# A four-layer graph network on one core: the last layer with narrow tiles in three bfloat16 parts and six blocks from streamed rows

## The chip, the core and the metric

The kernel runs on one core of a Trainium2 chip. Its engines work side by side, each through its own list of instructions in order: TensorE (PE, with its weight loads shown apart as PEld), VectorE (DVE), ScalarE (ACT), GpSimd (POOL) and SyncE (SP), which only issues transfers. The metric is device time of one execution in microseconds (us), as the median of several runs.

## What is computed

Four layers work on the same 2708 x 2708 adjacency matrix (sparse, densest in the first rows and columns, the diagonal always set) and on 2708 x 512 features. Each adds its result to its input and normalizes every row. The change lies in the last one:

```
bw = sign(weight)                     # 512 x 512
ba = maximum(sign(x), 0)              # 2708 x 512
xw = ba @ bw.T                        # small whole numbers
out = relu(adj @ xw)
x = layernorm(x + out)
```

`xw` holds whole numbers up to 512, which float16 holds exactly. `adj` is float32; the product `adj @ xw` is to keep its precision.

## The kernel before

The rows of the output are cut into 22 blocks of 128 (block 21 has 20). A block's columns of the transposed adjacency matrix are the stationary operands of its matmuls (128 source nodes x 128 output rows), the 512 features the moving ones. Since the matrix is sparse, layer 0 lists for every block, while it reads the matrix, which nodes have an edge to it. The listed rows are packed, 128 to a tile, and kept in SBUF for all layers (`packed[b]`, `tiles(b)` of them), together with index lists (`index[b]`). In each layer POOL then gathers the 128 feature rows of each packed tile from DRAM by an indirect transfer (`gathered`, L611). `ROOM[b]` is the number of gathered tiles of a block, 98 over blocks 1 to 21; `DIRECT[b]` names the blocks of nodes (0 and 1) that a block takes whole, without a list. Block 0 takes all nodes.

Some packed tiles are narrow. `SPLIT[b]` says how: in a block of kind "QQ" the first four gathered tiles hold only edges to one quarter of the block's rows each (32 rows), in "HH" the first two to one half each (64), "QH" and "HQ" have two quarters and one half. `span(b, i)` (L1326) gives the rows of tile i, `narrow_views` (L1343) the packed columns that matter, `whole_runs` (L1331) the runs of neighbouring tiles of full width, `in_turns` (L1360) the order "full width first, narrow last", and `last_of` (L1373) whether a matmul is the last one to its rows. Layers 0 to 2 use these: a narrow tile's matmul writes only the partitions `ps[r0:r1]`. The last layer before the change uses none of them and multiplies every tile at full width.

The last layer (from L1987) has two kinds of blocks. Blocks 0 to `WHOLE3` - 1 = 4 are summed over all 22 tiles of nodes: `whole_tile(j)` (L2060) loads 128 rows of `xw` and the first `W3` = 640 columns of the same rows of the transposed matrix (`aw`, four buffers), and adds to five PSUM banks (`whole`). The other blocks, in the order `order3` = 21, 5, 6, ... 20, are gathered: their tiles of `xw` come by `gather3(b)` (L2048) as float16 rows in DRAM that the transfer widens to float32r, into 11 buffers.

PE multiplies in float32r[...]. So a matrix tile is split by `halves_of` (L1994) into a high part (a cast on ACT, L1998) and the remainder (a subtraction on DVE, L1999), up to 512 columns at a time, `W3` for a streamed tile, in four buffers `parts`; every tile takes two matmuls (L2075 streamed, L2114 packed). The diagonal of a gathered block is added by two more (L2103), with a scaled identity matrix split in the same way (L2095, L2098) and the block's own rows (`xo`, L2087). `widened` (L2004) turns float16 rows into float32r, on ACT two times of three, else on DVE.

`finish3` (L2016) takes a block's sum: relu and addition of the input (L2022, which frees the PSUM bank), moments (L2024, L2026), and for two blocks at a time the inverse root and the scaling (L642 to L662, L2033 to L2043), and the store on SP.

The program text sets the order: five streamed tiles first (`AHEAD3`), then block by block; a counter `due` grows by `ROOM[b]`, and for each three gathered tiles (`FETCHES3`) one streamed tile follows the block. With the values before, the last of the 22 streamed tiles follows block 15. From then on each gathered block is finished together with a streamed one; what is left of these is finished after block 20. A scheduler may move an instruction ahead of others on its engine when the text's order is built, and then the order is fixed.

In layer 2, `gathered_2` (L1784) also uses memory that is no longer needed as places for gathered rows, one after another: two in `packed[0]`, and as many as fit in `early`, the tile that holds `packed[1]` to `packed[WHOLE3 - 1]`, once those blocks are done.

Of the kernel before, what the change touches and what calls it, by code (L numbers as in the profile page):

```python
# [8 lines left out]
F32 = mybir.dt.float32  # L9
# [10 lines left out]
P = 128  # L20
# [36 lines left out]
)  # L57


WHOLE3 = 5  # L60
AHEAD3 = 5
FETCHES3 = 3

# [444 lines left out]
def sparse_layers(ctx, tc, x, adj, adj_t, w0_t, b0, w_sa, a_sa, w_gcnb, b_gcnb, wa, ba, wb, bb, w3_t,  # L508
# [19 lines left out]
    def rows(b: int) -> int:  # L528
        return min(P, N - b * P)

    def direct(b: int):

        return tuple(range(NB)) if b == 0 else DIRECT.get(b, ())

    def tiles(b: int) -> int:
        return len(direct(b)) + ROOM[b]
# [71 lines left out]
    def own_by_itself(b: int) -> bool:  # L608
        return b not in direct(b)

    def gathered(pool, dst_w: int, src, b: int, i: int, dtype=F32):  # L611
        t = pool.tile([P, dst_w], dtype, tag="xg", name=f"xg{b}_{i}")
        nc.gpsimd.indirect_dma_start(  # L613
            out=t, out_offset=None, in_=src[:, :],
            in_offset=bass.IndirectOffsetOnAxis(ap=index[b][:, i : i + 1], axis=0),
        )
        return t
# [708 lines left out]
    def span(b: int, i: int):  # L1326

        t, spans = i - len(direct(b)), SPANS[SPLIT[b]]
        return spans[t][1:] if 0 <= t < len(spans) else (0, rows(b))
# [30 lines left out]
    def in_turns(b: int):  # L1360

        nd, n = len(direct(b)), narrow(b)
        mine = list(range(nd, nd + n))
        return [i for i in range(tiles(b)) if i not in mine] + mine
# [8 lines left out]
    def last_of(b: int, i: int, order):  # L1373

        r0, r1 = span(b, i)
        return all(
            span(b, j)[1] <= r0 or span(b, j)[0] >= r1 for j in order[order.index(i) + 1 :]
        )
# [607 lines left out]

    with tc.tile_pool(name="s_l3", bufs=11, reuse_waits="tile") as lp, \  # L1987
            tc.tile_pool(name="s_ps_w", bufs=1, reuse_waits="tile", space=PSUM) as ps_w, \
            tc.tile_pool(name="s_ps_3", bufs=3, reuse_waits="tile", space=PSUM) as ps_3:
        W3 = WHOLE3 * P  # L1990
        CH3 = 4
        PW = max(CH3 * P, W3)

        def halves_of(a, r: int, w: int, name: str):  # L1994

            p = lp.tile([P, 2, PW], F32R, tag="parts", name=f"p{name}", bufs=4)
            low, high = p[:r, 0, :w], p[:r, 1, :w]
            nc.scalar.copy(high, a)  # L1998
            nc.vector.tensor_tensor(low, a, high.bitcast(F32), op=ALU.subtract)  # L1999
            return p  # L2000

        turn = [0]

        def widened(t, r: int, name: str, tag: str = "wide", bufs: int = 4):  # L2004

            g = lp.tile([P, D], F32R, tag=tag, name=f"w{name}", bufs=bufs)
            turn[0] += 1
            if turn[0] % 3 == 0:
                nc.vector.tensor_copy(g[:r], t[:r])
            else:  # L2010
                nc.scalar.copy(g[:r], t[:r])
            return g

        moments = []

        def finish3(b: int, ps, more: bool):  # L2016

            m = rows(b)
            old = place_of_x(b)
            k = len(moments)  # L2020
            t = old[:, :D]
            nc.vector.scalar_tensor_tensor(t[:m], ps[:m], 0.0, t[:m], op0=ALU.max, op1=ALU.add)  # L2022
            st = small.tile([P, 6], F32, tag="st", name=f"st_3_{b}")
            nc.vector.bn_stats(st[:m], t[:m])  # L2024
            mv = moments[0][2] if k else lp.tile([P, 2, 2], F32, tag="mv3", name=f"mv_3_{b}", bufs=3)
            nc.vector.bn_aggr(mv[:m, k, :], st[:m])  # L2026
            moments.append((b, t, mv))
            if more:
                return
            n = len(moments)  # L2030
            rs = lp.tile([P, 2, 2], F32, tag="rs3", name=f"rs_3_{b}", bufs=2)
            mean, v = mv[:m, :n, 0], mv[:m, :n, 1]
            nc.vector.tensor_scalar(v, v, LN_EPS, None, op0=ALU.add)  # L2033
            rsqrt_of(rs[:m, 0, :n], v, m, n, f"3_{b}")
            nc.vector.scalar_tensor_tensor(
                rs[:m, 1, :n], mean, -1.0, rs[:m, 0, :n], op0=ALU.mult, op1=ALU.mult
            )
            for k, (b, t, _) in enumerate(moments):
                nc.scalar.activation(
                    t[:m], t[:m], AF.Identity, bias=rs[:m, 1, k : k + 1],  # L2040
                    scale=rs[:m, 0, k : k + 1],
                )
                nc.sync.dma_start(out[b * P : b * P + m, :], t[:m])  # L2043
            moments.clear()

        sources3 = {}

        def gather3(b: int):  # L2048
            sources3[b] = [gathered(lp, D, xw_rows, b, t, F32R) for t in range(ROOM[b])]

        order3 = [NB - 1, *range(WHOLE3, NB - 1)]
        gather3(order3[0])
        gather3(order3[1])


        whole = [ps_w.tile([P, D], F32, tag=f"w{b}", name=f"l3_{b}") for b in range(WHOLE3)]

        xw_direct = {0: xw0}

        def whole_tile(j: int):  # L2060
            r = rows(j)
            if j:
                g = lp.tile([P, D], F16, tag="xs", name=f"xs{j}", bufs=4)
                nc.sync.dma_start(g[:r], xw_rows[j * P : j * P + r, :])
                g = widened(g, r, f"s{j}", "wide" if j > 1 else "wide1", 4 if j > 1 else 1)
                if j == 1:
                    xw_direct[1] = g
            else:
                g = xw0
            a = lp.tile([P, W3], F32, tag="aw", name=f"aw{j}", bufs=4)  # L2070
            nc.sync.dma_start(a[:r], adj_t[j * P : j * P + r, :W3])
            p = halves_of(a[:r], r, W3, f"w{j}")
            for b in range(WHOLE3):
                for h in range(2):
                    nc.tensor.matmul(  # L2075
                        whole[b], p[:r, h, b * P : (b + 1) * P], g[:r, :],
                        start=(j == 0 and h == 0), stop=(j == NB - 1 and h == 1),
                    )
        j = 0
        while j < AHEAD3:  # L2080
            whole_tile(j)
            j += 1
        due = 0
        for at, b in enumerate(order3):
            m = rows(b)
            xo = lp.tile([P, D], F16, tag="xo", name=f"xo{b}", bufs=2)
            nc.sync.dma_start(xo[:m], xw_rows[b * P : b * P + m, :])  # L2087
            xo = widened(xo, m, f"o{b}")
            if at + 1 < len(order3) and at:
                gather3(order3[at + 1])  # L2090
            src = [xw_direct[j] for j in direct(b)] + sources3.pop(b)
            ps = ps_3.tile([P, D], F32, tag="mm", name=f"l3_{b}")

            dp = lp.tile([P, 2, P], F32R, tag="dp", name=f"dp{b}", bufs=2)
            nc.scalar.activation(  # L2095
                dp[:m, 1, :m], ident[:m, :m], AF.Copy, scale=dia_own[:m, b : b + 1]
            )
            nc.vector.scalar_tensor_tensor(  # L2098
                dp[:m, 0, :m], ident[:m, :m], dia_own[:m, b : b + 1],
                dp[:m, 1, :m].bitcast(F32), op0=ALU.mult, op1=ALU.subtract,  # L2100
            )
            for h in range(2):
                nc.tensor.matmul(  # L2103
                    ps[:m], dp[:m, h, :m], xo[:m, :], start=(h == 0), stop=False
                )
            for i0 in range(0, tiles(b), CH3):
                n = min(CH3, tiles(b) - i0)
                p = halves_of(
                    packed[b][:, i0 : i0 + n, :].rearrange("p n i -> p (n i)"), P, n * m,
                    f"{b}_{i0}",  # L2110
                )
                for i in range(n):
                    for h in range(2):
                        nc.tensor.matmul(  # L2114
                            ps[:m], p[:, h, i * m : (i + 1) * m], src[i0 + i],
                            start=False, stop=(i0 + i == len(src) - 1 and h == 1),
                        )
            pending = bool(moments)
            finish3(b, ps, not pending and b not in (order3[0], order3[-1]))
            if j == NB and whole and len(moments) == 1:  # L2120
                finish3(WHOLE3 - len(whole), whole.pop(0), False)
            due += ROOM[b]
            while j < NB and due >= FETCHES3:
                whole_tile(j)
                j += 1
                due -= FETCHES3
        while whole:
            finish3(WHOLE3 - len(whole), whole.pop(0), len(whole) % 2 == 1)
# [77 lines left out]
```

## Time and profile before

| | us |
|---|---|
| median of 3 runs | 1006.92 (1006.87 to 1007.9) |
| profiled execution | 1015.66 |
| its span, first to last instruction | 1013.9 |
| layer 2, 580 to 889 us of the span | 309 |
| last layer, 889 us to the end | 124.9 |
| PE busy over the span | 867.5 |
| DVE | 654.6 |
| ACT | 381.2 |
| POOL | 513.0 |

Durations of single instructions come from the profiled execution, which is 8.7 us longer than the median. "Busy" is the time in which an engine runs an instruction; matmuls overlap in the records, so their cost is read from the distance between starts. The "idle before" of an instruction names what its engine waited for last; "issue" is a wait for nothing that the profile shows, and can be a transfer.

The lines of the page that are the last layer's costliest:

```profile
L2075 PE MATMUL l<-ws,pw 128*128 128x512 f32 (+1 forms) x210 | 52.0, 401 | 3.7 <-DVE pw L1999 3.7
L2075 PEld LDWEIGHTS l<-ws,pw 128*128 128x128 f32 (+1 forms) x210 | 40.4, 194 | 14.0 <-DVE pw L1999 4.6
L613 POOL DMA_INDIRECT xg<-xw_rows,i x70 | 71.4, 1020 | 39.9 <-issue 16.5
```

Columns: line, engine, operation, tile written and tiles read, shapes, count; then busy time and mean ns of one; then the engine's idle time just before them and its main cause.

### The profile page before, as it was taken

Reading aid. Unit: us, or ns where it says so; the run is one execution under the profiler, and the core shown is the slowest. Engines: PE = TensorE matmul, PEld = TensorE weight load, DVE = VectorE, ACT = ScalarE, POOL = GpSimd, SP = SyncE. Lnnn points to the kernel's source line nnn. Section 1 sums busy time; section 2 is a strip of 40 time slices with the busy share of each in tenths; the row PEclk is TensorE's granted clock in tenths of the full one; section 3 lists DMA queues with packets and bytes.
Section 4 is the critical chain, followed back from the end, with each engine's and each line's share of the span. In section 5 each row is a group of like instructions: output and inputs, shape, how many; then the busy total and the mean of one; then the engine's idle time right before and its main releaser. Section 6 shows DMA issues by size and latency. Waiting matters only on the chain.

```text
span 1013.9 us, 12803 instructions
## 1 busy us (share of the span) xinstructions
PE 867.5 (86%) x3659; PEld 458.7 (45%) x3659; DVE 654.6 (65%) x2538; ACT 381.2 (38%) x822; POOL 513.0 (51%) x579
## 2 busy tenths in 40 slices
PE   1888889659587977989999988998999999699983
PEld 0444444212122324455555544453555555378762
DVE  5889797717366863546455436666888777556765
ACT  2665555100000012545445433333444333254654
POOL 2677888567666533646434034453454320066761
PEclk9898889879798988999999998999999999889986
DMA  9999895467676634766645266676786551299985
GB/s 288 332 330 313 293 299 162 142 197 215 189 228 202 199 122 132 216 198 207 199 150 165 80 235 239 225 272 219 261 320 224 176 176 44 82 308 331 310 233 169
DMA packets 93557, 220.06 MB, mean 217 GB/s; under 512 B 13660, under 2 KB 28364, under 8 KB 93476
## 3 DMA queue, kind: packets, MB, share of 16 engines
q0 software_dynamic: 43008, 127.61, 42.1%
q1 hardware_dynamic: 38520, 76.78, 22.3%
q10 hardware_dynamic: 11948, 14.76, 4.4%
q8 instruction: 31, 0.51, 0.2%
q14 instruction: 50, 0.41, 0.1%
HBM read 178.21 MB, written 31.71 MB: 207 GB/s over the span
## 4 chain that ended last, share of the span: by engine, by line
PE 63%; DVE 15%; issue 6%; DMA 6%; another core or an unknown queue 5%; ACT 3%; POOL 1%; ACTq 0%; DVEq 0%; SPq 0%; POOLq 0%
PE l L1369 11%; PE h L1595 7%; PE e L1820 6%; PE a L1820 6%; PE l L2075 4%; PE y L1106 4%; PE pg L1868 4%; PE l L2114 3%; PE pc L1868 3%; DMA xg<-x_rows,i 2%; PE e L1628 2%; PE px L1929 2%; PE a L1629 2%; DVE s_mask L874 1%
## 5 line engine op out<-in xcount | busy, mean ns | idle before, releaser
L613 POOL DMA_INDIRECT xg<-x_rows,i x98 | 94.8, 967 | 113.4 <-PE l L1369 65.7
L1072 POOL DMA_INDIRECT a<-in_adj_t_dram,row_at x98 | 111.0, 1132 | 59.2 <-DVE deg L817 24.0
L613 POOL DMA_INDIRECT xg<-y_rows,i x98 | 97.5, 995 | 50.3 <-issue 21.8
L1106 PE MATMUL y<-s_w,xt 128*128 128x512 f32 (+1 forms) x176 | 96.8, 702 | 0.0
L1369 PE MATMUL l<-xg,a 128*32 128x512 f32 (+3 forms) x196 | 83.2, 657 | 12.1 <-DMA xg<-y_rows,i 11.8
L613 POOL DMA_INDIRECT xg<-xw_rows,i x70 | 71.4, 1020 | 39.9 <-issue 16.5
L1796 POOL DMA_INDIRECT xg<-x_rows,i x60 | 59.9, 999 | 61.8 <-ACT ae L1551 18.0
L1595 PE MATMUL h<-s_wsa,xt 128*128 128x256 f32 (+3 forms) x352 | 83.5, 391 | 5.2 <-ACT xt L1590 5.0
L1796 POOL DMA_INDIRECT a<-x_rows,i x38 | 36.9, 970 | 93.3 <-DVE mask L1554 38.0
L1595 PEld LDWEIGHTS h<-s_wsa,xt 128*128 128x128 f32 (+1 forms) x352 | 65.4, 190 | 30.6 <-ACT xt L1590 14.0
L809 ACT ACTIVATE unused<-arow 128x1408 uint8<-128x1408 f32 (+3 forms) x44 | 58.3, 1325 | 2.4 <-DMA x_rows<-s_zero 1.7
L1106 PEld LDWEIGHTS y<-s_w,xt 128*128 128x128 f32 (+1 forms) x176 | 37.3, 223 | 43.4 <-issue 43.3
L2075 PE MATMUL l<-ws,pw 128*128 128x512 f32 (+1 forms) x210 | 52.0, 401 | 3.7 <-DVE pw L1999 3.7
L1820 PE MATMUL a<-xg,a 128*32 128x512 f32 (+2 forms) x120 | 50.9, 626 | 4.2 <-DMA xg<-x_rows,i 4.2
L1820 PE MATMUL e<-xg,ae 128*32 128x512 f32 (+2 forms) x120 | 47.9, 601 | 0.9 <-ACT ae L1556 0.9
L642 ACT ACTIVATE rsqs<-mv 128x1 f32<-128x1 f32 (+2 forms) x56 | 11.3, 201 | 94.8 <-DVE mv L671 48.9
L2075 PEld LDWEIGHTS l<-ws,pw 128*128 128x128 f32 (+1 forms) x210 | 40.4, 194 | 14.0 <-DVE pw L1999 4.6
L1868 PE MATMUL pg<-s_wg,pt 128*128 128x256 f32 (+1 forms) x176 | 44.9, 397 | 1.3 <-ACT pt L1856 1.3
L895 PE MATMUL find<-s_sides,s_mask 128*128 128x5 bf16 (+1 forms) x462 | 15.7, 166 | 34.8 <-DVE s_mask L891 25.0
L667 DVE BATCH_NORM_STATS2 st<-t 128x6 f32<-128x512 f32 (+1 forms) x66 | 45.3, 686 | 0.3
L1369 PEld LDWEIGHTS l<-xg,a 128*32 128x32 f32 (+3 forms) x196 | 19.6, 148 | 53.2 <-issue 33.0
L673 POOL TENSOR_TENSOR rs<-mv,s_neg_half 128x1 f32<-128x1 f32 (+1 forms) x22 | 12.9, 588 | 60.5 <-DVE mv L671 51.1
(306 smaller groups left out, 1965.6 us busy)
## 6 DMA issues: line engine op xcount, KB each, us to landing
arow<-in_adj_dram SPq DMA_DIRECT2D x21, 704.0 KB
arow<-in_adj_dram SPq DMA_DIRECT2D x21, 650.0 KB
x_rows<-f SPq DMA_DIRECT2D x40, 256.0 KB
aw<-in_adj_t_dram SPq DMA_DIRECT2D x21, 320.0 KB
y_rows<-yt ACTq DMA_DIRECT2D x20, 256.0 KB
x_rows<-h SPq DMA_DIRECT2D x19, 257.0 KB
f<-in_x_dram SPq DMA_DIRECT2D x19, 256.0 KB
h_own<-x_rows SPq DMA_DIRECT2D x19, 256.0 KB
```

The costliest lines, as they stand in the source:

```text
L613: nc.gpsimd.indirect_dma_start(out=t, out_offset=None, in_=src[:, :], in_offset=bass.IndirectOffsetOnAxis(ap=index[b][:, i : i + 1], axis=0),)
L667: nc.vector.bn_stats(st[:m], t[:m])
L809: nc.scalar.activation(unused[:m, : ar.shape[1]], ar, AF.Copy, accum_out=row_sums[:m, b, h : h + 1])
L1072: nc.gpsimd.indirect_dma_start(out=packed[b][:, t + len(direct(b)), :], out_offset=None, in_=adj_t, in_offset=bass.IndirectOffsetOnAxis(ap ...
L1106: nc.tensor.matmul(ps[:m], xt[:, k, :m], w0[:, k, :], start=(k == 0), stop=(k == KC - 1))
L1369: nc.tensor.matmul(ps[r0:r1], weights, moving, start=(i == order[0]), stop=last_of(b, i, order))
L1595: nc.tensor.matmul(ps, xt[:, k, :m], w[:, k, :], start=(k == 0), stop=(k == KC - 1))
L1796: nc.gpsimd.indirect_dma_start(out=g, out_offset=None, in_=x2_rows[:, :], in_offset=bass.IndirectOffsetOnAxis(ap=index[b][:, t : t + 1], a ...
L1820: nc.tensor.matmul(ps[r0:r1], weights, moving, start=(i == order[0]), stop=last_of(b, i, order))
L1868: nc.tensor.matmul(ps, pt[:, k, :m], w[:, k, :], start=(k == 0), stop=(k == KC - 1))
L2075: nc.tensor.matmul(whole[b], p[:r, h, b * P : (b + 1) * P], g[:r, :], start=(j == 0 and h == 0), stop=(j == NB - 1 and h == 1),)
L2114: nc.tensor.matmul(ps[:m], p[:, h, i * m : (i + 1) * m], src[i0 + i], start=False, stop=(i0 + i == len(src) - 1 and h == 1),)
```

## The change

Six parts:

- `WHOLE3` becomes 6: block 5 is now summed from streamed rows, with blocks 0 to 4; `W3` is 768; sixteen blocks are gathered, with 65 gathered tiles instead of 70. `early` also holds `packed[5]`, and one more place for gathered rows fits in it in layer 2.
- `gathered` takes a tag and a number of buffers.
- Gathered rows of narrow tiles stay float16 (`xh`, 12 buffers); those of full-width tiles are widened as before (`xg`, 8 buffers). Full-width tiles are gathered first.
- Streamed tiles of the matrix are loaded into four stretches of `early` instead of buffers of their own.
- Full-width packed tiles are split in two as before, in the runs that `whole_runs` gives. Narrow ones are split into three bfloat16 parts: a cast (ACT), a subtraction (DVE), a cast (ACT), a subtraction (DVE), and three matmuls each, which write the tile's own rows only; the first part of all narrow tiles, then the second, then the third.
- The gathered blocks' PSUM banks are two instead of three.

```diff
-WHOLE3 = 5
+WHOLE3 = 6
...
-    def gathered(pool, dst_w: int, src, b: int, i: int, dtype=F32):
-        t = pool.tile([P, dst_w], dtype, tag="xg", name=f"xg{b}_{i}")
+    def gathered(pool, dst_w: int, src, b: int, i: int, dtype=F32, tag="xg", bufs=None):
+        t = pool.tile([P, dst_w], dtype, tag=tag, name=f"{tag}{b}_{i}", bufs=bufs)
...
-            tc.tile_pool(name="s_ps_3", bufs=3, reuse_waits="tile", space=PSUM) as ps_3:
+            tc.tile_pool(name="s_ps_3", bufs=2, reuse_waits="tile", space=PSUM) as ps_3:
...
         def gather3(b: int):
-            sources3[b] = [gathered(lp, D, xw_rows, b, t, F32R) for t in range(ROOM[b])]
+            nd = len(direct(b))
+            sources3[b] = {
+                i: gathered(
+                    lp, D, xw_rows, b, i - nd, *((F16, "xh", 12) if span(b, i) != (0, rows(b))
+                    else (F32R, "xg", 8)),
+                )
+                for i in in_turns(b) if i >= nd
+            }
...
+        streamed = [early.rearrange("p n i -> p (n i)")[:, k * W3 : (k + 1) * W3] for k in range(4)]
...
-            a = lp.tile([P, W3], F32, tag="aw", name=f"aw{j}", bufs=4)
+            a = streamed[j % 4]
...
-            for i0 in range(0, tiles(b), CH3):
-                n = min(CH3, tiles(b) - i0)
+            for i0, n in whole_runs(b, CH3):
                 p = halves_of(
...
-                            start=False, stop=(i0 + i == len(src) - 1 and h == 1),
+                            start=False, stop=h == 1 and last_of(b, i0 + i, order_),
                         )
+            if narrow(b):
+                p = lp.tile([P, 3, P], BF16, tag="thirds", name=f"p{b}_n", bufs=2)
+                left = lp.tile([P, P], F32, tag="left", name=f"r{b}", bufs=1)
+                mine = []
+                for i0, r0, w, a in narrow_views(b):
+                    n = a.shape[1]
+                    nc.scalar.copy(p[:, 2, r0 : r0 + n * w].rearrange("p (n i) -> p n i", n=n), a)
+                    nc.vector.tensor_tensor(
+                        left[:, r0 : r0 + n * w].rearrange("p (n i) -> p n i", n=n), a,
+                        p[:, 2, r0 : r0 + n * w].rearrange("p (n i) -> p n i", n=n),
+                        op=ALU.subtract,
+                    )
+                    mine += range(i0, i0 + n)
+                nc.scalar.copy(p[:, 1, :], left)
+                nc.vector.tensor_tensor(p[:, 0, :], left, p[:, 1, :], op=ALU.subtract)
+                for h in (2, 1, 0):
+                    for i in mine:
+                        r0, r1 = span(b, i)
+                        nc.tensor.matmul(
+                            ps[r0:r1], p[:, h, r0:r1], src[i], start=False, stop=h == 0
+                        )
```

More of the change, by code (lines that the diff above doesn't have):

```diff
@@ L2090, in sparse_layers @@
                 gather3(order3[at + 1])
-            src = [xw_direct[j] for j in direct(b)] + sources3.pop(b)
+            src = sources3.pop(b)
+            src.update((i, xw_direct[c]) for i, c in enumerate(direct(b)))
+            order_ = in_turns(b)
             ps = ps_3.tile([P, D], F32, tag="mm", name=f"l3_{b}")
```

## The prediction

> **What bounds the kernel now.** I read the chain of waits first, then the busy time by stage, and then the last layer's own order of instructions. All changed instructions lie in the last layer, from 889 us of the span to its end, apart from one more place for gathered rows in the layer before it.
>
> The page's chain, its shares by engine; then the stages (length, busy time and count of PE, PEld, DVE, ACT, POOL, granted PE clock, DMA share, GB/s):
>
> ```profile
> PE 63%; DVE 15%; issue 6%; DMA 6%; another core or an unknown queue 5%; ACT 3%; POOL 1%; ACTq 0%; DVEq 0%; SPq 0%; POOLq 0%
> ```
>
> ```profile
> 889.00:982.00 93.00, 89.27 (x369) 71.00 (x370) 59.38 (x148) 50.52 (x101) 64.73 (x63) 0.96 1.07 306
> 982.00:1013.90 31.90, 15.90 (x54) 11.94 (x53) 19.47 (x79) 13.23 (x26) 6.68 (x8) 0.67 0.56 176
> ```
>
> Up to 982 us PE is the bound (89.3 of 93 us) with the DMA engines full beside it (share 1.07); DVE has a third of its time free. After 982 PE is half idle at a low clock, and DVE is busy 19.5 of the 24.7 us to its last instruction at 1006.65: the tail belongs to DVE. Now PE's timeline (start, length, instruction, idle before it and its releaser):
>
> ```profile
> 889.02 4.63 PE L2075 MATMUL l<-xw,pw 128*128 128x512 f32 x10 [3.27 <-DVE pw L1999]
> ...
> 939.40 2.56 PE L2075 MATMUL l<-ws,pw 128*128 128x512 f32 x10 [0.47 <-DVE pw L1999]
> ...
> 944.52 2.43 PE L2075 MATMUL l<-ws,pw 128*128 128x512 f32 x10
> 946.79 0.62 PE L2103 MATMUL l<-wo,dp 128*128 128x512 f32 x2
> ...
> 972.51 4.05 PE L2075 MATMUL l<-ws,pw 128*128 128x512 f32 x10 [3.24 <-DVE pw L1999]
> ...
> 979.25 2.58 PE L2075 MATMUL l<-ws,pw 20*128 20x512 f32 x10
> ...
> 993.51 0.61 PE L2103 MATMUL l<-wo,dp 128*128 128x512 f32 x2
> 998.32 1.22 PE L2114 MATMUL l<-xw,p 128*128 128x512 f32 x2 [4.19 <-DVE p L1999]
> ```
>
> A whole tile of ten matmuls takes 946.79-944.52 = 2.27 us: 0.227 us for one float32r matmul over 512 columns. PE is late in four places: at the start (bound by the end of layer 2), at 939, at 972, and at 998. The wait at 972 is a transfer: ACT sat idle before its split of that streamed tile, though its four buffers had been read:
>
> ```profile
> 970.87 0.72 ACT L1998 CAST pw<-aw 128x640 fp32r<-128x640 f32 x1 [4.39 <-issue]
> ```
>
> The wait at 998 is DVE's: it ran block 20's split only then, behind sums and moments of other blocks:
>
> ```profile
> 997.58 0.69 DVE L1999 TENSOR_TENSOR p<-a,p 128x512 fp32r<-128x512 f32 x1
> ```
>
> That is where a late split holds PE. POOL's 70 gathers start every 1.24 us and end at 992.7, so POOL is close behind PE without holding it.
>
> [...] on layer 1's narrow tiles (a float32 matmul leaves two records, so x8 are four matmuls):
>
> ```profile
> 424.24 1.02 PE L1369 MATMUL l<-xg,inc 128*128 128x512 f32 x2
> 425.19 1.06 PE L1369 MATMUL l<-xg,incn 128*32 128x512 f32 x8
> 426.18 1.12 PE L1628 MATMUL e<-h,e 20*128 20x512 f32 x2
> ...
> 566.02 2.05 PE L1369 MATMUL l<-xg,incn 128*32 128x512 f32 x6
> 568.00 0.66 PE L1588 MATMUL xt1p<-s_ident,f 128*128 128x128 f32 x4
> ```
>
> Two records at full width cost 0.86 us (861.34 to 862.20 in layer 2), and four narrow matmuls together 0.99: shared, with 0.13 us for the change of mode. A block with two widths took 1.98, twice that. [...] Here the ten matmuls after the wait at 972 took 4.05 us instead of 2.27. [...]
>
> **The change part by part.**
> *Matmuls.* Before: 22 tiles x 5 blocks x 2 halves = 220 streamed, 17 x 2 = 34 for the diagonals, 84 tiles x 2 = 168: 422 x 0.227 = 95.6 us. After: 22 x 6 x 2 = 264, 16 x 2 = 32, and 32 full-width tiles x 2 = 64: 360 x 0.227 = 81.5 us. The 45 narrow tiles go in three bfloat16 passes. A pass costs one bfloat16 matmul of 512 columns, 0.215 us (the four of line 1929 take 0.86), shared by the tiles of one width. Six blocks in quarters and six in halves: 3 x 0.215 + 0.13 = 0.78 us each, 9.3 us. Blocks 14, 16 and 19 mix widths and change mode six times: 6 x (0.215 + 0.13) = 2.07, 6.2 us. Sum 97.0: PE has 1.4 us more to do, not less. Bounds: if the mode's 0.13 us is paid in each pass, 12 x 0.26 = 3.1 more; if changes of mode cost nothing, 97.0 - 30 x 0.13 = 93.1.
> The order of the work changes too: by the counter of gathered tiles the last streamed tile now comes after block 16, not after block 15. Up to it: 336 x 0.227 + 4.65 + 2.33 + 4.14 = 87.3 us against 368 x 0.227 = 83.5. After it, blocks 17 to 20: 24 x 0.227 + 4.4 = 9.8 against 54 x 0.227 = 12.3.
> *Splits.* Streamed splits go from 640 to 768 columns: ACT 0.72 to 0.83 us by the slope of its rows (0.29 at 128, 0.62 at 512), DVE 0.83 to 0.96: 22 x 0.11 and 22 x 0.13, +2.4 and +2.9 us. The first delays the layer's start by 0.24 us on the path. A narrow block has ACT, DVE, ACT, DVE in a row, at 0.29 us each, and its full-width tiles in up to two runs: about 0.3 us more than now on each engine, 15 x 0.3 = 4.5; block 5's steps go, -2. So +5 us on ACT and +6 on DVE, hidden up to 982 by DVE's free 33 us; if that cover is gone it is rival C.
> *Transfers.* Streamed tiles grow by 22 x 64 KB = 1.4 MB; five gathers go (1.3 MB as written), 45 gathers write 128 KB instead of 256 (5.9 MB); block 5's own row load goes (0.1 MB). Of some 36 MB (22 x 0.46 streamed, 70 x 0.26 gathered, 17 x 0.13 and 22 x 0.26 for own rows and output) about 6 go. POOL issues 65 x 1.24 = 81 us instead of 87, and may run 20 tiles ahead instead of 11. That speaks for the waits at 939 and 972 to go: 0.47 + 0.3 + 3.24 + 1.78 (slow clock) = 5.8 us. I leave 1 us of them, the bounds being 0 and 5.8.
> *Buffers.* Streamed tiles now land in the old adjacency tiles, where layer 2 keeps gathered rows; its readers there are the matmuls of blocks 19 and 20, done by 862.2, while SP's first streamed load went at 870.23, behind a DVE step of layer 2. So nothing is late. ACT's splits stand in its order behind block 20's copy at 885.79, so an earlier load brings nothing. One PSUM bank less for gathered blocks: block b+2 waits for DVE's first read of block b. Up to the last streamed tile 2.7 us or more lie between; in the tail it can bite. One more gather place in layer 2: PE is busy 284 of 309 us there and POOL 110, so nothing.
> *Tail.* After the last streamed matmul DVE still has 4 gathered and 5 or 6 streamed blocks to sum and measure, as now 5 and 4 or 5, at about 1.3 us each (0.60 + 0.60 + 0.1): equal. PE has 2.5 us less, and would start warm. Of the 20.3 us from 981.83 to the last block's sum at 1002.13, 8 are stall and slow clock (12.3 are work). Bounds: -5 us if DVE's 5 idle us go, +3 if two blocks' more steps come last. I take -2.
>
> **Sum**, against the profiled execution (span 1013.9, 1015.66 with what lies around it): +0.24 + 3.8 - 4.8 - 2 = -2.8 us. The median of the runs is 1006.92, 8.7 us below the profiled one; I take the same difference there: 1004.1 us.
>
> **Rivals.**
> A. Transfers cease to matter and the tail runs warm: +4.0 - 5.8 - 5 = -6.8, 1000.1 us. For: 6 MB fewer and 9 more buffers. Against: DVE is the tail's engine and gets no less work.
> B. The late transfer stays, since gathers that run further ahead crowd the stream: +4.0 - 2 = +2.0, 1008.9 us. For: the DMA share was 1.42 at 955 to 958. Against: the bytes.
> C. Slower: the four-step split comes late. Alone it takes 4 x 0.29 + 0.2 = 1.4 us; with one foreign step of 0.7 us queued ahead at each of three hand-overs, 3.5 us. Its cover is the streamed work between two blocks, 6 x 2 x 0.227 = 2.7 us where one tile lies there and nothing in the tail. It decides once the split is ordered behind the previous block's sum. Price 3.5 - 2.7 = 0.8 on five blocks and 1.5 on three of the tail: +8.5, so +5.7, 1012.6 us. For: the DVE wait at 998 is this kind already. Against: two buffers let a split run a block ahead.
> D. The bfloat16 passes do not share the array: 135 x 0.215 = 29 us instead of 15.5, so +10.7, 1017.6 us. Against: layer 1's float32 tiles share it.
>
> **Chances.** Forecast 0.40, A 0.20, B 0.12, C 0.24, D 0.04. A difference under 0.2% (2 us) can't be told from none here. The forecast's own range is 1000 to 1008 (faster 0.30, same 0.09, slower 0.01); A is faster; B divides, 0.05 same and 0.07 slower; C and D are slower. Faster 0.50, same 0.14, slower 0.36. The range from 998 to 1013 leaves out D and the edges.
>
> **What would show it.** Right: 360 float32r matmuls in the layer; a quarter block's 12 narrow ones in about 0.8 us and a mixed block's 9 in about 2; no wait near 972 with ACT idle on a transfer; the last streamed matmul within 2 us of 981.8; POOL done by 980. Wrong: PE waiting on DVE's last narrow step (C), narrow matmuls one after another (D), or a layer 2 end that has moved by more than 1 us.

## The result: 1.0% slower, and the profile after

Beside the kernel before on one chip, the changed kernel took 1019.12 us (median of 13 runs) against 1008.5 (13 runs): ratio 1.0101, 95% interval 1.0077 to 1.0125, some 10 us slower. Forecast were 1004.1 us and a range that ended at 1013. The profiled execution took 1019.12 us, its span 1017.3.

The chain's shares by engine, on the page of the changed kernel, hardly differ from before:

```profile
PE 64%; DVE 14%; DMA 6%; issue 6%; another core or an unknown queue 5%; ACT 3%; POOL 1%; ACTq 0%; DVEq 0%; SPq 0%; POOLq 0%
```

The last layer by stage (length, busy time and count of PE, PEld, DVE, ACT, POOL, granted PE clock, DMA share, GB/s), cut at the same times as before:

```profile
889.00:982.00 93.00, 85.38 (x401) 59.78 (x400) 53.19 (x152) 45.59 (x108) 65.92 (x63) 0.94 0.83 249
982.00:1017.30 35.30, 19.61 (x88) 10.74 (x86) 23.83 (x98) 17.07 (x39) 0.00 (x0) 0.84 0.30 110
```

The layer starts 4 us earlier in this profile (884.98 instead of 889.02). In the first stage PE is less busy than before (85.4 us instead of 89.3) and DMA's share has fallen from 1.07 to 0.83. DVE and ACT do less too. So no engine became the bound; something stops them all. PE's timeline says where:

```profile
884.98 5.38 PE L2084 MATMUL l<-xw,pw 128*128 128x512 f32 x12 [2.90 <-DVE pw L1999]
...
902.70 1.08 PE L2124 MATMUL l<-xg,p 128*128 128x512 f32 x4
903.71 0.82 PE L2146 MATMUL l<-xh,p_n 128*32 128x512 f16 x9
905.59 0.38 PE L2146 MATMUL l<-xh,p_n 128*32 128x512 f16 x1 [1.06 <-issue]
909.08 1.29 PE L2146 MATMUL l<-xh,p_n 128*32 128x512 f16 x2 [3.12 <-issue]
911.88 8.76 PE L2084 MATMUL l<-ws,pw 128*128 128x512 f32 x24 [1.51 <-issue]
920.48 0.62 PE L2114 MATMUL l<-wo,dp 128*128 128x512 f32 x2
...
966.53 3.03 PE L2084 MATMUL l<-ws,pw 128*128 128x512 f32 x12 [0.45 <-issue]
...
990.66 0.73 PE L2114 MATMUL l<-wo,dp 128*128 128x512 f32 x2
...
1001.36 0.73 PE L2124 MATMUL l<-xg,p 128*128 128x512 f32 x2 [1.25 <-DVE p L1999]
```

PE stops inside block 6, the first narrow block, after nine of its twelve narrow matmuls, and goes on at a low clock (granted 0.50 from 908 to 917 us): 24 streamed matmuls take 8.6 us (911.88 to 920.48), not the 24 x 0.227 = 5.45 of the prediction's price. The other engines' lines from the timeline of the same stop:

```profile
914.10 0.43 DVE L2009 CAST wo<-xo 128x512 fp32r<-128x512 f16 x1 [7.55 <-remote]
914.10 0.62 ACT L2011 CAST ws<-xs 128x512 fp32r<-128x512 f16 x1 [8.54 <-issue]
914.40 0.94 POOL L613 DMA_INDIRECT xg<-xw_rows,i  x1 [3.29 <-remote]
```

DVE, ACT and POOL go on within 0.3 us of each other. The stop and the slow clock cost some 10 us: from the ninth narrow matmul to the end of the streamed tiles behind block 6 lie 16 us (904.5 to 920.5), of which six are work.

### The profile page after: what moved, and what is told of

Same layout as the page of the kernel before. It is cut to its first block, busy times and chain, and to the rows that moved or that the text cites. A ratio compares the mean times of both kernels' runs of the same rounds, so it can differ in the third digit from the quotient of the medians.

```text
span 1017.3 us, 12974 instructions
## 1 busy us (share of the span) xinstructions
PE 864.9 (85%) x3732; PEld 446.3 (44%) x3732; DVE 653.7 (64%) x2566; ACT 384.1 (38%) x849; POOL 511.8 (50%) x574
## 4 chain that ended last, share of the span: by engine, by line
PE 64%; DVE 14%; DMA 6%; issue 6%; another core or an unknown queue 5%; ACT 3%; POOL 1%; ACTq 0%; DVEq 0%; SPq 0%; POOLq 0%
PE l L1369 13%; PE h L1595 7%; PE l L2084 7%; PE a L1820 6%; PE e L1820 6%; PE pg L1868 3%; PE pc L1868 3%; PE y L1106 3%; PE l L1430 2%; PE e L1628 2%; DVE s_mask L874 2%; PE l L2146 2%; DMA a<-x_rows,i 2%; PE a L1629 2%
## 5 line engine op out<-in xcount | busy, mean ns | idle before, releaser
L613 POOL DMA_INDIRECT xg<-x_rows,i x98 | 94.9, 969 | 108.2 <-PE l L1369 61.5
L1106 PE MATMUL y<-s_w,xt 128*128 128x512 f32 (+1 forms) x176 | 94.1, 685 | 1.1 <-ACT xt L1098 1.1
L1796 POOL DMA_INDIRECT a<-x_rows,i x44 | 42.9, 974 | 96.6 <-DVE mask L1554 37.9
L1796 POOL DMA_INDIRECT xg<-x_rows,i x54 | 53.8, 997 | 53.8 <-ACT ae L1551 15.1
L2084 PE MATMUL l<-ws,pw 128*128 128x512 f32 (+1 forms) x252 | 64.4, 407 | 3.3 <-issue 2.9
L2084 PEld LDWEIGHTS l<-ws,pw 128*128 128x128 f32 (+1 forms) x252 | 47.8, 194 | 20.4 <-issue 9.9
L613 POOL DMA_INDIRECT xh<-xw_rows,i x45 | 48.2, 1070 | 14.0 <-issue 12.2
L1820 PE MATMUL a<-xg,a 128*32 128x512 f32 (+2 forms) x108 | 44.9, 619 | 4.2 <-DMA xg<-x_rows,i 4.2
L1820 PE MATMUL e<-xg,ae 128*32 128x512 f32 (+2 forms) x108 | 42.7, 600 | 1.2 <-issue 1.2
L1868 PE MATMUL pc<-s_wg,pt 128*128 128x258 f32 (+1 forms) x176 | 42.7, 384 | 0.0
```

What stands on the lines that cost most here:

```text
L613: nc.gpsimd.indirect_dma_start(out=t, out_offset=None, in_=src[:, :], in_offset=bass.IndirectOffsetOnAxis(ap=index[b][:, i : i + 1], axis=0),)
L1106: nc.tensor.matmul(ps[:m], xt[:, k, :m], w0[:, k, :], start=(k == 0), stop=(k == KC - 1))
L1796: nc.gpsimd.indirect_dma_start(out=g, out_offset=None, in_=x2_rows[:, :], in_offset=bass.IndirectOffsetOnAxis(ap=index[b][:, t : t + 1], a ...
L1820: nc.tensor.matmul(ps[r0:r1], weights, moving, start=(i == order[0]), stop=last_of(b, i, order))
L1868: nc.tensor.matmul(ps, pt[:, k, :m], w[:, k, :], start=(k == 0), stop=(k == KC - 1))
L2084: nc.tensor.matmul(whole[b], p[:r, h, b * P : (b + 1) * P], g[:r, :], start=(j == 0 and h == 0), stop=(j == NB - 1 and h == 1),)
```

## The experiments

Eighteen runs of twelve kernels follow, in five groups, each group on one chip with the kernel before beside it. The chips are of two kinds, and both kernels differ between them by 5 to 6%: on some the kernel before takes about 1010 us (the result above, and groups 2 to 4), on others about 960 (groups 1 and 5). Two chips of each kind stand behind the groups (groups 2 and 3 ran on the same one). So ratios are compared, and profiles only within a kind. How finely: the kernel before, run as an experiment beside itself, gave 0.9964, 0.9981 and 0.9993. On the 1010 us chips a difference of 0.4% is no finding, whatever its interval.

The last layer in the profiles, in us, read from PE's timeline: A from the first streamed matmul to the end of the last one, with PE's waits in it; B from there to PE's end; C from there to the span's end.

| chip | kernel | ratio, 95% | A (waits) | B | C | A+B+C |
|---|---|---|---|---|---|---|
| 1010 | before, first profile | | 92.8 (3.7) | 20.3 | 11.8 | 124.9 |
| 1010 | before_b | 0.9964 [0.9940, 0.9988] | 91.9 (4.1) | 20.9 | 11.9 | 124.7 |
| 1010 | before_c | 0.9981 [0.9957, 1.0006] | 91.0 (3.4) | 21.5 | 11.9 | 124.4 |
| 1010 | changed, first profile | 1.0101 [1.0077, 1.0125] | 105.8 (7.1) | 12.1 | 14.4 | 132.3 |
| 1010 | again2 | 1.0102 [1.0054, 1.0150] | 111.8 (8.4) | 14.7 | 14.4 | 140.9 |
| 1010 | short2 | 1.0001 [0.9977, 1.0026] | 93.3 (0.3) | 14.8 | 14.4 | 122.4 |
| 1010 | before18 | 1.0074 [1.0051, 1.0096] | 100.8 (11.1) | 20.6 | 11.8 | 133.2 |
| 1010 | w6again | 0.9998 [0.9975, 1.0021] | 96.9 (0.5) | 11.4 | 17.2 | 125.5 |
| 1010 | n5ahead | 1.0108 [1.0072, 1.0143] | 105.9 (16.1) | 18.5 | 14.0 | 138.4 |
| 1010 | short_wide | 0.9955 [0.9923, 0.9988] | 92.9 (1.3) | 13.0 | 14.3 | 120.3 |
| 960 | before_d | 0.9993 [0.9978, 1.0009] | 87.0 (0.0) | 17.7 | 11.9 | 116.6 |
| 960 | again | 1.0063 [1.0039, 1.0087] | 92.9 (0.0) | 13.7 | 14.4 | 121.0 |
| 960 | short | 1.0073 [1.0053, 1.0092] | 92.2 (0.0) | 13.7 | 14.4 | 120.3 |
| 960 | w6 | 1.0095 [1.0074, 1.0117] | 95.8 (0.0) | 9.8 | 16.8 | 122.5 |
| 960 | n5 | 1.0034 [1.0022, 1.0047] | 87.1 (2.0) | 19.6 | 11.8 | 118.5 |
| 960 | wide2 | 1.0046 [1.0026, 1.0065] | 91.3 (0.0) | 13.2 | 14.3 | 118.8 |

The profiled execution of again2 took 1030.78 us, 9 us above its median: its row shows where it stops, but overstates by how much. The sizes of effects are taken from ratios and medians.

### Group 1, a 960 us chip: is the stop chance, and which part costs?

**again**: the changed kernel, no edit.

> The changed kernel once more, to see whether the stop of PE inside block 6 (some 10 us between 904 and 921 us of the span) comes back. Theory S (it belongs to the change: POOL runs up to 20 gathers ahead, the DMA engines fill[...]): the stop is there again at block 6, 5 to 11 us, and the time is 8 to 12 us above the kernel before. Theory R (a chance stop of the DMA engines, as the one at 966 to 971 us in the trace of before): it is elsewhere or gone in the new trace, and the time is still some 10 us above, from other causes.

Measured: 1.0063, no stop. I took that for chance (theory R). It was not, as group 3 shows: this was the other kind of chip. But some 5.6 us of loss are there without any stop.

**short**: the changed kernel with 8 and 4 buffers for gathered tiles.

```diff
-                    lp, D, xw_rows, b, i - nd, *((F16, "xh", 12) if span(b, i) != (0, rows(b))
-                    else (F32R, "xg", 8)),
+                    lp, D, xw_rows, b, i - nd, *((F16, "xh", 8) if span(b, i) != (0, rows(b))
+                    else (F32R, "xg", 4)),
```

> The change with 8 float16 and 4 widened gather buffers instead of 12 and 8, so that POOL can run two blocks ahead as before and not three and more. Theory S: the stop at block 6 shrinks to under 3 us and the time falls by 4 to 8 us against the changed kernel. Theory W or R: within 2 us of the changed kernel.

Measured: 1.0073, no different from again. On this chip the buffers make no difference that can be told.

**w6**: six streamed blocks alone: the kernel before with `WHOLE3 = 6`, two PSUM banks and the streamed tiles in `early`.

> Six streamed blocks alone: gathered tiles all at full width in float32r with 11 buffers, as before; streamed tiles in the old adjacency tiles, two PSUM banks for gathered blocks. PE's sum is 6.4 us more than before. Theory W: 5 to 9 us slower than before. Theory S: no stop at block 6, so the cost is PE's alone, 3 to 7 us slower; what lies between that and the 10 us of the whole change is the narrow part's.

Measured: 1.0095, the costliest of the four. **n5**: narrow thirds alone: the changed kernel with `WHOLE3 = 5` and three PSUM banks.

> The narrow tiles in three bfloat16 parts alone: five streamed blocks as before, three PSUM banks for gathered ones. PE's sum is 5 us less than before. Theory W (six streamed blocks are what costs: 44 more streamed matmuls against 16 fewer of block 5, +6.4 us on PE): 2 to 6 us faster than before. Theory S (gathers that run ahead hold up the start): the stop is here too, and the time is 2 to 8 us above the kernel before.

Measured: 1.0034, where fewer matmuls should have gained; both theories missed. In its profile PE has 1.9 us less to do in A, but waits 2.0 us there, all of it for gathers, as here:

```profile
885.08 0.81 PE L2146 MATMUL l<-xh,p_n 128*32 128x512 f16 x9 [0.79 <-DMA xh<-xw_rows,i]
```

POOL issues n5's 70 gathers in 91.8 us without a pause of a microsecond, one each 1.33 us, and PE has caught up with them. B is 1.9 us longer than in before_d, and why stays open. So the two parts don't add up (1.0095 and 1.0034 alone, 1.0063 together). Six streamed blocks are the larger loss on this chip, by PE's added work, and beside them the narrow tiles win some of it back.

### Group 2, a 1010 us chip

**before_b**: the kernel before, no edit.

> The kernel before, unchanged, with a profile on the chip of the other runs. The prediction took 5.8 us of PE's waits for late transfers in the last layer of its profile as something that the kernel before has in every execution, and credited 4.8 us of them to the change. Theory R (chance): this profile has under 2 us of PE's waits on transfers between the last layer's first streamed tile and its last, and that stretch takes 86 to 89 us instead of the 92.8 us in the first profile. Theory L (they belong to the kernel): 4 us or more of such waits, at the streamed tiles and the gathered blocks, and 92 us or more.

Measured: 4.1 us of waits in A. **before_d**, in group 5 on a 960 us chip, has none:

> The kernel before once more. On a chip of some 960 us: PE waits under 1 us between the last layer's first and last streamed tile, and from the layer's start to the end of the span 116 to 119 us. On a chip of some 1010 us: 3 to 4 us of waits and 124 to 125 us, as in three profiles; ratio beside itself 0.996 to 1.002.

PE's timeline of before_d shows the first streamed matmuls, the last ones and the only wait after the layer's start:

```profile
843.12 4.63 PE L2075 MATMUL l<-xw,pw 128*128 128x512 f32 x10 [3.26 <-DVE pw L1999]
...
927.51 2.58 PE L2075 MATMUL l<-ws,pw 20*128 20x512 f32 x10
...
945.71 0.73 PE L2114 MATMUL l<-xw,p 128*128 128x512 f32 x2 [3.33 <-DVE p L1999]
```

So the late transfers that the prediction credited belong to the 1010 us chips: three profiles there have 3.4 to 4.1 us of waits in A.

**nonarrow**: the changed kernel without line 2146. It leaves out the narrow tiles' 135 matmuls (15 blocks; the expectation miscounts both), so its sums lack these edges; the gathers and splits remain.

> The changed kernel without the matmuls of the narrow tiles in the last layer (14 blocks' 144 narrow matmuls are left out, gathers and splits stay). Theory W (the last layer is bound by PE, and the narrow part costs 15.5 us as the prediction summed, or about 18.7 us with the entry and the exit of each block): 15 to 19 us less than the changed kernel, so a ratio of 0.986 to 0.991 to the kernel before. Theory S (the gathers and their transfers set the pace): less than 8 us gained, because POOL's gathers and the splits are unchanged.

Measured: 1.0283 [1.0237, 1.0329]. With 135 matmuls fewer it is some 28 us slower than the kernel before, and by the ratios (1.0283 against 1.0102 in again2, on the same chip) some 18 us *slower* than the changed kernel, against both theories' numbers. What the edit did besides: no matmul reads the `xh` tiles any more, so their buffers are free at once and POOL need not wait for PE. It issued gathers without a pause from 887 to 928 us. Meanwhile, all engines' timeline:

```profile
932.84 0.62 ACT L2011 CAST ws<-xs 128x512 fp32r<-128x512 f16 x1 [19.56 <-remote]
932.88 0.43 DVE L2009 CAST wo<-xo 128x512 fp32r<-128x512 f16 x1 [19.47 <-remote]
933.18 0.95 POOL L613 DMA_INDIRECT xg<-xw_rows,i  x1 [4.59 <-remote]
...
935.23 1.22 PE L2084 MATMUL l<-ws,pw 128*128 128x512 f32 x2 [17.30 <-DVE pw L1999]
```

It is a joint stop like the first one, after 32 gathers in a row, and more than twice as long. That brought back the theory that gathers which run ahead cause it.

**n5ahead**: as n5, with each block's thirds split one block ahead and the passes of a mixed block ordered by width:

```diff
-                for h in (2, 1, 0):
-                    for i in mine:
+            by_width = [[i for i in mine if span(b, i)[1] - span(b, i)[0] == w] for w in (32, 64)]
+            for h, i in [(h, i) for g in by_width for h in (2, 1, 0) for i in g]:
```

> Narrow thirds with five streamed blocks (as n5), with the narrow tiles split into thirds one block ahead, before the finish of the block before, and with the mixed blocks' passes ordered by width. If n5 lost its expected 2.5 us to the four-step split being late in the tail (3.0 us of PE's waits for p_n and p there): 3 to 5 us less than n5, ratio 0.994 to 1.000 to the kernel before. If the split was not what cost: within 1 us of n5, ratio 1.003.

Measured: 1.0108, with 16 us of waits in A. What an earlier split is worth can't be told from it: n5 ran on the other kind of chip, and the stop, after 21 gathers in a row, covers it. **w4**: the kernel before with `WHOLE3 = 4`.

> The kernel before with four streamed blocks instead of five (block 4 gathered in f32r, all else as before). Theory W: PE loses 44 matmuls of a streamed block and gains 18 of a gathered one, 26 by 0.227 us = 5.9 us less work, and the stretch is bound by PE: 4 to 6 us faster, ratio 0.994 to 0.996. Theory G (the gathers of POOL, six more at 1.24 us, and the packed splits on ACT and DVE set the pace once fewer blocks are streamed): same or slower, ratio 1.000 to 1.006.

Measured: 0.9962 [0.9935, 0.9990], the same as before_b in the same group, so no gain is shown. PE had 28 matmuls fewer, but waited 9.4 us in A (more gathers) and 6.2 in B.

### Group 3, a 1010 us chip: the buffers again

**again2** and **short2** are the kernels of again and short; **before_c** is the kernel before.

> The changed kernel once more. On a chip of some 960 us: no wait of PE in the streamed stretch, ratio 1.005 to 1.008. On a chip of some 1010 us: theory R (the 10 us stop at block 6 was chance): under 5 us of waits in the stretch, ratio 1.003 to 1.007. Theory S (the stop belongs to the change where the chip's transfers are slower): 6 to 10 us of waits before the last streamed tile, one of them at blocks 6 and 7, ratio 1.008 to 1.012.

> The changed kernel with 8 and 4 buffers for the gathered tiles instead of 12 and 8, as in short. On a chip of some 1010 us: theory S (gathers that run ahead of the streamed loads hold these up): 3 to 8 us less than the changed kernel beside it, fewer waits in the streamed stretch. Theory R: within 2 us of it. On a chip of some 960 us both give the same as short: within 2 us.

> The kernel before once more, with a profile. Its time beside itself also says how far two equal kernels can differ on one chip (0.996 on the last one). On a chip of some 960 us: theory R, PE waits under 1 us between the last layer's first and last streamed tile, stretch 86 to 88 us, and from the layer's start to the end of the span 116 to 119 us, so that the changed kernel's 121.0 us there is 2 to 5 us longer. On a chip of some 1010 us: 4 us of waits, stretch 92 us, 124.8 us in all, as in two profiles.

Measured: 1.0102 and 1.0001. With fewer buffers the loss is gone, 10.5 us at the medians (1021.63 to 1011.14). again2 stops at the very place of the first profile; these are PE's lines of again2, then of short2:

```profile
906.69 0.82 PE L2146 MATMUL l<-xh,p_n 128*32 128x512 f16 x9
908.65 0.38 PE L2146 MATMUL l<-xh,p_n 128*32 128x512 f16 x1 [1.14 <-issue]
910.75 1.31 PE L2146 MATMUL l<-xh,p_n 128*32 128x512 f16 x2 [1.72 <-issue]
```

```profile
906.47 0.83 PE L2146 MATMUL l<-xh,p_n 128*32 128x512 f16 x12
907.23 5.74 PE L2084 MATMUL l<-ws,pw 128*128 128x512 f32 x24
912.80 0.62 PE L2114 MATMUL l<-wo,dp 128*128 128x512 f32 x2
```

What differs is POOL. Its first gather of the layer and the first one after a pause, in again2, short2 and before_c:

```profile
888.42 1.32 POOL L613 DMA_INDIRECT xg<-xw_rows,i  x1 [7.53 <-DMA xw_rows<-xw]
...
917.43 0.94 POOL L613 DMA_INDIRECT xg<-xw_rows,i  x1 [2.72 <-remote]
```

```profile
887.44 0.99 POOL L613 DMA_INDIRECT xg<-xw_rows,i  x1 [7.54 <-DMA xw_rows<-xw]
...
905.42 0.95 POOL L613 DMA_INDIRECT xg<-xw_rows,i  x1 [1.79 <-PE l L2124]
```

```profile
885.68 0.99 POOL L613 DMA_INDIRECT xg<-xw_rows,i  x1 [7.57 <-DMA xw_rows<-xw]
...
901.75 0.94 POOL L613 DMA_INDIRECT xg<-xw_rows,i  x1 [2.36 <-PE l L2103]
```

again2 issues 20 gathers in a row, short2 12 and before_c 11: as many as each has buffers (12 + 8, 8 + 4, 11). In short2 and before_c POOL then pauses until PE has read a buffer; in again2 its pause is already part of the stop. The shorter rows have a price of their own: in short and short2 PE waits 4.30 us before the layer's first matmul, instead of 2.90 in again and again2.

**f35**: the kernel before with `FETCHES3 = 3.5`, so that the last streamed tile follows block 18.

> The kernel before with one streamed tile for every 3.5 gathered tiles instead of 3, so that the last streamed tile comes after block 18 and not after block 15. If the tail behind the last streamed tile is what the last layer loses (blocks 17 to 20 took 20 us there with 11 us of matmuls, PE waiting 4 to 6 us for a split and its clock falling): 3 to 6 us faster than before, ratio 0.994 to 0.997. If the finishes of the five streamed blocks set the end: they start later by what the streamed tiles are later, same or 1 to 3 us slower.

Measured: 1.0047 [1.0021, 1.0072]. PE ended 5 us after the last streamed tile instead of 21, but 17.5 us then passed to the span's end (C). So the hoped-for gain isn't there: the finishes on DVE and ACT set the end, and they start later. A loss of 0.5% is hardly above what the kernel before shows beside itself.

### Group 4, a 1010 us chip: is it the buffers alone?

**before18**: the kernel before with 18 gather buffers instead of 11. Nothing is narrow, nothing float16, five blocks streamed; the streamed tiles lie in `early` to make room.

```diff
-            sources3[b] = [gathered(lp, D, xw_rows, b, t, F32R) for t in range(ROOM[b])]
+            sources3[b] = [gathered(lp, D, xw_rows, b, t, F32R, 18) for t in range(ROOM[b])]
```

> The kernel before with 18 buffers for the gathered tiles instead of 11 (the streamed tiles lie in the space of the first blocks' packed tiles, to make room). Theory S (the gathers run ahead and hold up the streamed rows, whatever else is changed): on a chip of some 1010 us POOL's first pause in the last layer comes after some 20 gathers instead of some 13, the second streamed row after the start is cast more than 20 us after its issue (13.9 us in the kernel before), PE waits 6 to 12 us in the stretch, ratio 1.004 to 1.010. If float16 or the narrow tiles are needed for the stop: 0.998 to 1.002. On a chip of some 960 us no difference by either.

Measured: 1.0074, 11 us of waits in A. Its PE timeline has the stop behind the first gathered blocks, where the streamed tiles should follow:

```profile
896.63 2.45 PE L2116 MATMUL l<-xg,p 128*128 128x512 f32 x10
906.57 3.78 PE L2077 MATMUL l<-ws,pw 128*128 128x512 f32 x8 [7.49 <-DVE f L2022]
```

POOL issued 18 gathers, as many as its buffers, before its first pause. A deeper buffer makes the kernel before slower by most of what the change does. That the streamed tiles lie in `early` is not the reason: they do so in w6again and short2 too, which have no such stop. The expected late cast came one row later than said: the second streamed row after the start is cast 15.0 us after its load's issue, the third 20.0 us.

**w6again**: w6 on this kind of chip.

> Six streamed blocks alone, as w6, with the 11 gather buffers of the kernel before. By PE's sum 28 matmuls more, 6.4 us: ratio 1.004 to 1.009 on any chip. If on a chip of some 1010 us the transfers' waits cover PE's extra work: 1.000 to 1.003 there, and 1.009 on one of some 960 us as measured.

Measured: 0.9998, against 1.0095 on the 960 us chip. A is 5 us longer than before, not 9, since PE's waits in it fall to 0.5 us. Why they fall, no run shows.

**short_wide**: short with the passes ordered by width, as in n5ahead; **wide2** is the same kernel in group 5, on a 960 us chip.

> The changed kernel with 8 and 4 gather buffers and the passes of the three mixed blocks ordered by width (two changes of width instead of six in each). The mixed blocks' nine matmuls take 1.5 us instead of 2.0: 1 to 2 us less than short, ratio 0.997 to 1.000 on a chip of some 1010 us, 1.004 to 1.007 on one of some 960 us.

> The same kernel as short_wide. If it is faster than the kernel before on a chip of some 1010 us by what its profile has less in the last layer (120.3 against 124.6 us): ratio 0.995 to 0.998, below the kernel before beside itself. If 0.9955 was the spread of the measurement: 0.998 to 1.002. On a chip of some 960 us: 1.004 to 1.007.

Measured: 0.9955 at equal medians (1010.78 and 1010.88), which is within what the kernel before shows beside itself, and 1.0046. The nine matmuls of a mixed block take 1.52 us instead of 1.97, from start to start; block 14 in again and in wide2:

```profile
914.66 2.04 PE L2146 MATMUL l<-xh,p_n 128*32 128x512 f16 x9
916.63 3.03 PE L2084 MATMUL l<-ws,pw 128*128 128x512 f32 x12
```

```profile
918.06 1.59 PE L2146 MATMUL l<-xh,p_n 128*32 128x512 f16 x9
919.58 3.01 PE L2084 MATMUL l<-ws,pw 128*128 128x512 f32 x12
```

On the 1010 us chips the kernel is better than the changed one, by the buffers, but not for certain better than the kernel before; on the 960 us chip it is slower than the kernel before, and its interval overlaps that of again.

**n5_short**: n5ahead with 8 and 4 buffers.

> n5ahead (narrow thirds, five streamed blocks, split a block ahead, passes by width) with 8 and 4 gather buffers. Theory S: n5ahead lost its 16 us of waits to the gathers' run-ahead, so 8 to 14 us less than n5ahead on a chip of some 1010 us: ratio 0.994 to 1.001. On a chip of some 960 us as n5 or a little less, 1.000 to 1.003. If the split a block ahead was what cost: still 1.008 to 1.011 on a chip of some 1010 us.

Measured: 1.0028 [1.0004, 1.0053], from 1.0108: most of n5ahead's loss was the buffers' too.

## Why the prediction was wrong

**The step that failed: "Transfers".** It said that POOL "may run 20 tiles ahead instead of 11. That speaks for the waits at 939 and 972 to go", and took 4.8 us off. The run-ahead was seen rightly (20 gathers in a row) and its sign was wrong. On a 1010 us chip it makes a new stop: 10.5 us at the medians between again2 and short2, which differ in the number of buffers alone, and 7 us between before18 and the kernel before. Rival B named this mechanism ("gathers that run further ahead crowd the stream") with a chance of 0.12, but priced it as the old waits that stay (+2.0) and not as a new one. "Against: the bytes" was no argument: the changed kernel's stop comes with DMA half idle (below).

The credit itself was real on these chips, once the run-ahead is gone: short2 waits 0.3 us in A where the kernel before waits 3.4 to 4.1. Its reasons need not be the ones given: w6again waits only 0.5 us, with the 11 buffers of before and without narrow tiles, so without bytes saved by float16. On a 960 us chip nothing was there to be credited. One reading was off besides: the ten matmuls after the wait at 972 take 3.89 us from start to start (972.51 to 976.40, at a mean granted clock of 0.59), 4.05 being the length of their record, so the waits were worth 5.6 us and not 5.8.

**A second term was too small: 0.78 us for a narrow block.** It counted one change of mode (from full-width matmuls to narrow ones or back) at 0.13 us; there are two, into the narrow matmuls and out. PE's lines of again, block 7:

```profile
867.06 0.63 PE L2124 MATMUL l<-xw,p 128*128 128x512 f32 x2
867.53 0.63 PE L2124 MATMUL l<-xg,p 128*128 128x512 f32 x2
868.09 0.83 PE L2146 MATMUL l<-xh,p_n 128*32 128x512 f16 x12
868.85 5.75 PE L2084 MATMUL l<-ws,pw 128*128 128x512 f32 x24
874.44 0.61 PE L2114 MATMUL l<-wo,dp 128*128 128x512 f32 x2
```

Two matmuls at full width take 0.47 us (867.06 to 867.53), but 0.56 before the narrow ones: 0.09 on the way in. The narrow ones take 0.76. The 24 streamed ones take 5.59 where 24 x 0.227 = 5.45: 0.14 on the way out. In w6, on the same chip and without narrow tiles, 24 of them take 5.44:

```profile
861.82 5.60 PE L2077 MATMUL l<-ws,pw 128*128 128x512 f32 x24
867.26 0.61 PE L2105 MATMUL l<-wo,dp 128*128 128x512 f32 x2
```

So the block costs 0.99 us, 0.21 more than summed. The 0.09 and 0.14 us are what the two changes of mode cost here. Up to the last streamed tile lie nine blocks of one width (9 x 0.21 = 1.9 us) and two mixed ones (9 matmuls in 1.97, 2.2 with both ends, instead of 2.07: 0.3). The prediction's +3.8 for this stretch (its products are off by up to 0.2 us each, 360 x 0.227 being 81.7, but the differences stand) becomes +6.0, and A of again is 92.9 - 87.0 = 5.9 us longer than that of before_d.

Point by point, the rest:

- *Matmuls*: 360 in float32r and 135 narrow ones, and the passes share the array (the 12 narrow matmuls of block 7 in again take 0.76 us; one after another, by rival D's price of 0.215 us each, they would take 2.58): right, rival D is out. That its 1017.6 us lies near the measured time is chance.
- *Splits* and rival C: no split is late up to the last streamed tile on a 960 us chip (no waits in A), and the wait in the tail is 1.24 us, down from 3.33. Their cover held; C is out for the changed kernel. (n5's PE does wait 1.6 us in the tail for a narrow tile's parts.) The start moved by -0.4 us (2.90 us of idle before it instead of 3.27), not +0.24.
- *Buffers*: two PSUM banks and streamed tiles in `early` bring no wait into A on a 960 us chip: right. What the extra place in layer 2 is worth can't be told from the profiles.
- *Tail*: -2 was forecast, -1.5 came (again and before_d: B 17.7 to 13.7, C 11.9 to 14.4). PE did start the tail at full clock (granted 1.00 from 990 to 1002 us in the changed kernel's first profile, against 0.79 from 982 to 990 in that of the kernel before). The reason given was half wrong: PE saves 4, and one more streamed block finished behind PE gives 2.5 back.

On a 960 us chip the sum closes but for some 1 us: +5.9 - 1.5 = +4.4 us in the profiles, +5.6 at the medians. On a 1010 us chip short2 shows what is left without the stop. Beside the three profiles of the kernel before, its A is 0.5 to 2.3 us longer, B 5.5 to 6.7 shorter and C 2.5 longer, and it waits 1.0 us more before the layer's first matmul: 1 to 1.5 us less in the profiles, and +0.1 at the ratio (interval -2.3 to +2.6). So there the change without its deeper buffers can't be told from none, and the stop, the 10.5 us from short2 to again2, is the whole loss.

**What stays open.** Why a long row of gathers stops the other engines, and why only on one kind of chip: in again, on a 960 us chip, POOL issues all 65 gathers without a pause of a microsecond, and nothing stops. From 900 to 905 us of the changed kernel's first profile, when ACT and DVE have stood since 897 (ACT until 904.2, DVE until 905.6) and PE is about to stop, the DMA queues show POOL's gathers alone (packets, MB, share of 16 engines):

```profile
q0 software_dynamic: 308, 0.69, 48.0%
```

SP's queue moves nothing, and has nothing left: from 884 to 900 us it was given five stretches of the matrix, four rows of `xs` and four of `xo`, 2.9 MB in all, and moved 2.9 MB. So SP's queue wasn't shut out, and with the engines at 48.0% bandwidth isn't what is short here. In before18 it may be: from 896 to 906 us, around its stop, POOL's gathers take 91.0% of the engines and SP's transfers 13.5%, so that crowding as in rival B isn't excluded there. That the two stops have one mechanism is not shown; what is shown is that deeper gather buffers bring both.

In the changed kernel PE itself stops between matmuls whose operands earlier passes had already read, and its weight loads start 1.4 us apart, waiting for nothing the profile shows:

```profile
907.70 0.10 PEld L2146 LDWEIGHTS <-p_n 128*32 128x32 bf16 x1 [3.42 <-issue]
909.10 0.10 PEld L2146 LDWEIGHTS <-p_n 128*32 128x32 bf16 x1 [1.30 <-issue]
910.50 0.29 PEld L2084 LDWEIGHTS l<-ws,pw 128*128 128x128 f32 x1 [1.29 <-issue]
```

Instructions that come late might look like this, but the two DMA queues of the kind "instruction" (q8 and q14, 80 packets in the whole span) show no packet between 888 and 920 us, so the trace does not support it. Late signals are another candidate. The traces have a hint of them: just before ACT, DVE and POOL go on, no queue moves a packet (913.0 to 914.1 us here, 916.5 to 917.1 in again2, 931.5 to 932.8 in nonarrow), so that data they may have waited for had been moved by then. No run tests it.

## What to carry to other kernels

The depth of a gather buffer is also the brake on the engine that issues the gathers (20 went out in a row in again2, 12 in short2, 11 in before_c and 18 in before18, as many as each had buffers): when a change frees memory, keep the number of gathers that may run ahead as it was, and try depth as an edit of its own. A wait found in one profile is credited only after a second profile, of another chip if possible, shows it again; here the same 4 us were there on one kind of chip and absent on the other. Matmuls on part of the array pay for the change of mode on the way in and on the way out (here 0.09 and 0.14 us), so a short narrow group must save more than both.

## What was not expected of the hardware

- Two kinds of chip: the last layer of the kernel before starts at 843 us on one and at 879 to 889 on the other, and takes 116.6 or 124.4 to 124.9. The same change costs 0.6% on one, by PE's work, and 1.0% on the other, by a stop.
- Leaving 135 matmuls out made the changed kernel some 18 us slower: with no matmul left to read them, the buffers no longer held the gathers back, 32 went out in a row, and the stop grew from some 7 us to over 17.
- A change of mode costs 0.09 us in and 0.14 out; with two widths, grouping the passes by width saves 0.45 of 1.97 us.
- After the stop the PE clock stays low: 24 matmuls take 8.6 us instead of 5.45, which is 3.2 us of the stop's price of some ten. With PE all but idle from 904.5 us on, the granted clock falls to 0.50 at 907, after some 2.6 us, and is back at 1.00 by 918.
